# Rank and gather-index work of two batch groups due most of a batch sooner, order planned anew

## The chip, the cores and the metric

One core of one Trainium2 chip. The metric is device time in microseconds: the median of three runs of the kernel before was 818.91 us (818.41 to 819.88).

## The reference, cut to what matters

Sixteen batches `b` of 512 tokens with 512 features, and a context of 512 x 1024 for each batch.

```python
# x: (16, 512, 512), ctx: (16, 512, 1024), lens: (16, 512) int32
h     = rmsnorm(layernorm(x), g_res) @ W_in.T + b_in
u     = rmsnorm(ctx, g_init)[..., :512]            # scaled by constants
s     = scan over the tokens: s[t] = exp(-dt) * s[t-1] + u[t]
bidx  = cumsum(lens, axis=1) - 1                   # where a patch ends
mark  = zeros.at[bidx].set(1)
plug  = clip(cumsum(mark, axis=1) - 1, 0, 511)     # rank of each token's patch
x     = x + h + s[plug]                            # a gather by row
y     = layernorm(x);  yp = y shifted by one token
r     = sigmoid((mu_r*y + (1-mu_r)*yp) @ W_r.T)
k     = relu((mu_k*y + (1-mu_k)*yp) @ W_k.T) ** 2
out   = x + r * (k @ W_v.T)
```

The part that the change touches is `plug`: from the sorted end positions of a batch, the rank of every token, which is the row that the gather reads for it.

## The kernel before

**Tiles and stages.** A batch is four blocks `j` of 128 tokens, or four blocks `c` of 128 features. Each of the four products of a batch (`a` with W_in, `k`, `r`, `v`) is four groups of 12 matmuls of 128x128 by 128x512: float32 is split into a high and a low half, and a group sums high x high, high x low and low x high, four matmuls each. The names of the profile: `pa`, `pk`, `pr`, `pw` are the results of the four products in PSUM, `xh`, `m`, `ka` their operands in two halves, `cx` the context tiles that hold the scan, `pc` the carry between the blocks of the scan, `dr` the scan in DRAM, `x` the batch itself, `y` its second norm, `tr` that norm transposed, `pv` the mix with the token before, `sg` the sigmoid.

**Staging.** In period `i` the kernel computes `k`, `r` and `v` of batch `i`, the product `a` of batch `i+1`, and loads, squares and scans the context of batch `i+2`. For batch `b` the gather is four indirect transfers `x<-dr,plug` that GpSimd issues (`gather`, one for each `j`); they add rows of `dr` to `x[:, j]`. VectorE then adds `pa` (`a_end`), which also frees the PSUM bank of `pa`, and takes the second norm (`norm2`).

**Ranks.** `plugs(b0, n)` makes the index of `n` batches at once: the first batch alone, then batches 1 to 3, and 4 to 7, 8 to 11 and 12 to 15. For four batches it is: four one-hot comparisons `oh` on VectorE (128x512, each in a temporary tile of its own), 16 small matmuls that count (`cp<-ohj,oh`), four VectorE instructions that clip and sum (`bm`), one matmul with a triangle (`cp<-bm,small`), and three VectorE instructions that end in the integer index (`pf`, `pf`, `plug`). The groups of batches 8 and 12 are added to the program behind the store of batches 4 and 7.

**Order.** No instruction stands where the loops put it. `Plan` takes every piece with its engines, an estimated cost, what it reads and writes, and a due time `late`, which is worked back from its users and from the buffers. `SHIFT` adds a fixed number of microseconds to the due time of all pieces of a stage, named by kind and batch. `Plan.order` then runs a list schedule by these due times and its costs, and picks as it goes: which engine takes a piece that two engines can do (`LO`: the low half, a subtraction, on VectorE or on GpSimd), and which buffer a tile gets. There are 8 temporaries (`tmp`, 128x512), 16 operand tiles (`op`), 3 tiles for `x`, and PSUM is 4 banks for products (`ps`) and 4 for transposes (`tr`); the free buffer with the lowest number is taken. The order so found is then fixed on each engine:

```python
            if p.at is not None:
                p.late = p.at
            elif p.engines[0][0] == PE and p.due < INF:
                p.late = max(p.late, p.due - EASE)
            p.late += SHIFT.get(p.stage, 0.0)
```

Each engine works through its own queue in that order and waits at the head of it. Loads on SyncE carry one more wait, for a TensorE piece that stood some microseconds before them in the plan.

Of the kernel before, what the change touches and what calls it, by code (L numbers as in the profile page):

```python
# [289 lines left out]
class InOrder:  # L290
# [98 lines left out]
    ("sq", 4): 2.2,  # L389
    ("stat1", 4): 2.5,  # L390
    ("store", 4): -10.4,
}
ONLY = {
    ("rv", 0): 0,
# [939 lines left out]
```

## Time and profile before

| | |
|---|---|
| median of 3 runs | 818.91 us (818.41 to 819.88) |
| profiled execution, own time | 820.11 us |
| its span, first to last instruction | 818.3 us |
| granted TensorE clock, mean | 0.989 |
| TensorE matmul busy | 793.1 us (97%) |
| VectorE busy | 603.9 us (74%) |
| ScalarE busy | 485.1 us (59%) |
| GpSimd busy | 442.3 us (54%) |

In the profile PE is TensorE's matmuls and PEld its weight loads, DVE is VectorE, ACT ScalarE, POOL GpSimd, SP SyncE. Nearly all instructions have line 300, which is the helper that records them, so groups are told apart by the tiles that they write and read, with the numbers of batch and buffer left out. `x<-dr,plug` is the gather, `x<-bc` the transfer that adds the bias to `x`. The clock is given as a share of full speed. In the answers with a wait, the arrow names what ended it.

### The profile page before, as it was taken

The page shows a single profiled execution, that of the slowest core. Times are in us where ns is not written, and L with a number is a line of the kernel's source. Part 1 is how long each engine was busy: PE and PEld are TensorE (multiplying, and loading weights), DVE is VectorE, ACT ScalarE, POOL GpSimd, SP SyncE. Part 2 cuts the span into 40 slices and gives each one's busy share as a digit, 9 for nine tenths or more (in the row PEclk, how much of TensorE's full clock was granted, in tenths as well). Part 3 has the DMA queues.
Part 4 walks back from the last instruction along what each step waited for, and adds up shares of the span by engine and source line. Part 5 has one row for each costly group of instructions (what it writes and reads, how often), then busy time and mean ns, then how long its engine had stood idle before and what let it go on. Part 6 is the DMA issues. An engine that isn't in the chain of part 4 may idle for free.

```text
span 818.3 us, 11141 instructions
## 1 busy us (share of the span) xinstructions
PE 793.1 (97%) x3627; PEld 629.5 (77%) x3627; DVE 603.9 (74%) x1331; ACT 485.1 (59%) x950; POOL 442.3 (54%) x366
## 2 busy tenths in 40 slices
PE   7998998999999999999899999999989999999997
PEld 4776776877777888877678888887768888888885
DVE  6899798989789696777867678586966959564432
ACT  6937495555573757565476756647656565654550
POOL 2843675574767656552665566543566564561220
PEclk8999999999999999999999999999999999999999
DMA  9857485885685877673756866745577574430011
GB/s 322 269 91 260 101 236 144 283 224 155 142 241 155 175 200 194 168 217 111 208 126 171 224 155 208 153 168 146 150 216 170 199 139 170 91 80 16 2 52 51
DMA packets 52554, 134.69 MB, mean 165 GB/s; under 512 B 4752, under 2 KB 5264, under 8 KB 50576
## 3 DMA queue, kind: packets, MB, share of 16 engines
q1 hardware_dynamic: 35744, 102.39, 36.7%
q0 software_dynamic: 16608, 31.46, 23.8%
q8 instruction: 28, 0.46, 0.2%
q14 instruction: 30, 0.25, 0.1%
q10 hardware_dynamic: 144, 0.13, 0.0%
HBM read 85.73 MB, written 33.55 MB: 146 GB/s over the span
## 4 chain that ended last, share of the span: by engine, by line
PE 69%; DVE 13%; DMA 8%; issue 3%; POOL 3%; ACT 2%; SPq 0%; DVEq 0%; POOLq 0%; ACTq 0%
PE pk L300 18%; PE pr L300 17%; PE pw L300 17%; PE pa L300 14%; DMA x<-dr,plug 4%; DVE x L300 3%; PE tr L300 3%; DMA x<-x 3%; DVE cx L300 2%; DVE pv L300 2%; DVE sg L300 1%; PE pc L300 1%; DMA cx<-cx 1%; DMA out<-x 1%; POOL x L300 1%
## 5 line engine op out<-in xcount | busy, mean ns | idle before, releaser
L300 POOL TENSOR_TENSOR m<-pv,m 128x512 fp32r<-128x512 f32 x80 | 113.0, 1419 | 109.0 <-ACT m L300 50.4
L300 PE MATMUL pk<-m,whk 128*128 128x512 f32 x512 | 136.3, 401 | 6.8 <-DVE x L300 6.7
L300 PE MATMUL pa<-wha,xh 128*128 128x512 f32 x512 | 136.7, 404 | 4.9 <-DVE x L300 2.0
L300 PE MATMUL pw<-whv,ka 128*128 128x512 f32 x512 | 139.5, 399 | 0.4 <-ACT sg L300 0.4
L300 PE MATMUL pr<-whr,m 128*128 128x512 f32 x512 | 138.6, 397 | 0.0
L300 POOL DMA_INDIRECT x<-dr,plug x64 | 112.7, 1760 | 46.7 <-issue 15.7
L300 ACT ACTIVATE pv<-tr,om 128x384 f32<-128x384 f32 (+1 forms) x256 | 100.5, 487 | 41.6 <-PE tr L300 26.9
L300 DVE SCALAR_TENSOR_TENSOR pv<-tr,small,pv 128x511 f32<-128x511 f32 x128 | 95.0, 742 | 37.0 <-ACT pv L300 37.0
L300 PEld LDWEIGHTS pk<-m,whk 128*128 128x128 f32 x512 | 96.7, 191 | 33.0 <-DVE x L300 8.6
L300 PEld LDWEIGHTS pa<-wha,xh 128*128 128x128 f32 x512 | 96.8, 191 | 31.6 <-DVE x L300 3.2
L300 PEld LDWEIGHTS pr<-whr,m 128*128 128x128 f32 x512 | 95.2, 188 | 23.6 <-ACT kr L300 0.9
L300 PEld LDWEIGHTS pw<-whv,ka 128*128 128x128 f32 x512 | 94.6, 188 | 22.6 <-ACT sg L300 1.3
L300 ACT CAST m<-pv 128x512 fp32r<-128x512 f32 x128 | 76.3, 643 | 41.1 <-DVE pv L300 36.1
L300 ACT ACTIVATE sg<-pr 128x512 f32<-128x512 f32 x64 | 38.3, 600 | 96.4 <-PE pr L300 86.0
L300 DVE TENSOR_TENSOR ka<-kr,ka 128x512 fp32r<-128x512 f32 x52 | 39.8, 764 | 75.0 <-ACT ka L300 74.9
L300 ACT ACTIVATE y<-x,r 128x512 f32<-128x512 f32 x48 | 39.1, 815 | 73.0 <-DVE r L300 47.7
L300 DVE TENSOR_TENSOR sg<-pw,sg 128x512 f32<-128x512 f32 (+1 forms) x65 | 44.0, 678 | 41.6 <-PE pw L300 41.6
L300 ACT ACTIVATE junk<-cx 128x1024 bf16<-128x1024 f32 x64 | 67.5, 1055 | 7.4 <-DMA cx<-cx 7.1
L300 PE MATMUL pa<-wla,xh 128*128 128x512 f32 x256 | 71.1, 401 | 0.3 <-POOL wla L300 0.3
L300 PE MATMUL pk<-m,wlk 128*128 128x512 f32 x256 | 71.3, 403 | 0.0
L300 POOL TENSOR_TENSOR r<-r,mhalf 128x1 f32<-128x1 f32 x64 | 40.0, 627 | 57.2 <-DVE r L300 47.0
L300 PE MATMUL pw<-wlv,ka 128*128 128x512 f32 x256 | 70.5, 397 | 0.0
(116 smaller groups left out, 1276.8 us busy)
## 6 DMA issues: line engine op xcount, KB each, us to landing
cx<-cx SPq DMA_DIRECT2D x64, 512.0 KB, 6.0
dr<-cx SPq DMA_DIRECT2D x64, 256.0 KB, 4.4
out<-x SPq DMA_DIRECT2D x31, 512.0 KB, 2.7
x<-x SPq DMA_DIRECT2D x15, 1024.0 KB, 6.1
x<-bc POOLq DMA_DIRECT2D x14, 1024.0 KB, 8.1
raw<-xT SPq DMA_DIRECT2D x26, 512.0 KB, 6.1
wsa<-winT SPq DMA_DIRECT2D x2, 512.0 KB, 5.5
x<-x SPq DMA_DIRECT2D x4, 256.0 KB, 6.9
```

The source lines that it names most:

```text
L300: r = self._tc.keep_in_program_order(op(*args, **kwargs))
```

## The change

Two entries are added to `SHIFT`: all pieces of the rank and index work of batches 8 to 11 and of batches 12 to 15 get a due time 40 us sooner. No function changes, and no instruction is added or removed.

```diff
@@ SHIFT
     ("stat1", 4): 2.5,
     ("store", 4): -10.4,
+    ("plugs", 8): -40.0,
+    ("plugs", 12): -40.0,
 }
```

The plan is made anew with these due times, so other pieces change place too. As the two programs are built, TensorE's order is the same but for the 17 rank matmuls of each group. On VectorE, ScalarE, GpSimd and SyncE the order differs from period 5 to period 8 and again from period 9 to period 12, and is the same elsewhere. Ten subtractions move from VectorE to GpSimd (`m_1_3`, `ka_0` and `ka_1` of batches 6 and 10, `m_1_3` and `m_0_2` of batches 7 and 11; the first number is 1 for `k` and 0 for `r`, the last is `c`) and two from GpSimd to VectorE (`cl` of batches 8 and 12).

## The prediction

> **What bounds it now.** First the page: TensorE, and the chain is two thirds matmuls. A measurement of this kernel can tell about 0.2% (1.6 us) from no change.
>
> ```profile
> PE 793.1 (97%) x3627; PEld 629.5 (77%) x3627; DVE 603.9 (74%) x1331; ACT 485.1 (59%) x950; POOL 442.3 (54%) x366
> PE 69%; DVE 13%; DMA 8%; issue 3%; POOL 3%; ACT 2%; SPq 0%; DVEq 0%; POOLq 0%; ACTq 0%
> ```
>
> So only what stops TensorE counts. Stretches of 25 us show where that is, behind the first 275 us:
>
> ```profile
> core 0: us, PE busy (x) PEld busy (x) DVE busy (x) ACT busy (x) POOL busy (x), PEclk, DMA share, GB/s
> 375.00:400.00 25.00, 25.00 (x131) 20.14 (x130) 23.34 (x46) 13.37 (x29) 13.99 (x10) 1.00 0.50 133
> 400.00:425.00 25.00, 21.76 (x87) 17.11 (x86) 14.24 (x43) 15.81 (x27) 13.41 (x14) 0.93 0.76 204
> 425.00:450.00 25.00, 25.00 (x118) 20.44 (x117) 19.50 (x36) 13.80 (x29) 15.47 (x11) 1.00 0.60 152
> 600.00:625.00 25.00, 22.16 (x89) 17.43 (x88) 14.10 (x37) 15.88 (x28) 14.46 (x12) 0.93 0.63 158
> ```
>
> All other rows from 275 to 800 have 25.00 busy at clock 1.00. Both holes lie in the periods that prepare batches 8 and 12, whose ranks the change moves. Stretches of 2 us show the clock behind the first hole, then the timeline what leads to it:
>
> ```profile
> 410.00:412.00 2.00, 2.00 (x8) 1.56 (x8) 1.90 (x8) 2.00 (x4) 1.14 (x2) 0.73 0.85 289
> 412.00:414.00 2.00, 2.00 (x7) 1.51 (x6) 1.63 (x5) 1.94 (x4) 1.91 (x2) 0.50 0.31 119
> 414.00:416.00 2.00, 2.00 (x9) 1.63 (x8) 1.47 (x7) 1.97 (x5) 1.40 (x2) 0.91 0.00 0
> ```
>
> ```profile
> 388.08 1.21 DVE L300 CAST plug<-pf 128x16 int32<-128x16 f32 x1
> 389.58 1.70 POOL L300 DMA_INDIRECT x<-dr,plug  x1 [0.32 <-DVE plug L300]
> 399.34 1.55 POOL L300 DMA_INDIRECT x<-dr,plug  x1 [0.16 <-issue]
> 408.90 0.75 DVE L300 SCALAR_TENSOR_TENSOR x<-pa,rs,x 128x512 f32<-128x512 f32 x1 [3.70 <-DMA x<-dr,plug]
> 409.71 1.20 PE L300 MATMUL pk<-m,whk 128*128 128x512 f32 x4 [3.24 <-DVE x L300]
> ...
> 431.88 1.54 POOL L300 DMA_INDIRECT x<-dr,plug  x1 [0.17 <-issue]
> ```
>
> The index is ready at 389.3, the last gather goes out at 399.34 and lands 9.46 us later (the chain has that as one piece), VectorE adds `pa` only then, and TensorE waits for that PSUM bank. Batch 9, without rank work, has its four gathers out from 424.35 to 431.88, before its `pa` starts at 443.89. For batch 8, `pa` starts at 391.62: the first gather stands only 2.0 us before `pa`, not 19.5. The wait for the index itself is only 0.32 us; what costs is that the plan, expecting the index late, put the gathers behind subtractions on GpSimd.
>
> **Gain, step by step.** The period from one first `pr` matmul to the next is 47.21 us (419.75 to 466.96) and 47.22 in plain periods; 53.05 (366.70 to 419.75) and 52.95 (561.56 to 614.51) in the two with ranks. Excess: 5.84 + 5.74 = 11.58. Of it:
> - Idle: `pk` matmuls of 0.933 a four end at 406.30 and go on at 409.71, 3.41; at batch 12 601.47 to 604.47, 3.00.
> - Half clock behind it: nine fours take 10.04 where 9 x 0.933 = 8.39: 1.65 in each.
> - The rank matmuls, which stay: 382.60 to 386.95 holds four fours (3.73) in 4.35: 0.62 in each.
> - Rest: 0.16 and 0.47 (small waits for VectorE at `pa`).
>
> With the gathers out early, all but the 2 x 0.62 can go: 10.34. That they will be: in the order as built, all four stand directly behind the `sq` power of batch 9 (372.5 in this trace, some 2 us later by then), with one addition between, ahead of all `m` subtractions of batch 7. Batch 7's four with that addition took 9.3 us (322.89 to 332.2); so the fourth leaves at about 385 and, at the median 5.7 us, lands near 391, and its `pa` block ends at 403.5. The bias transfer before it (out at 362.39, 8.1 us) goes up to 3.2 us later, behind two `ka` subtractions; still 6 us clear.
>
> **What moves, and its cover.** The rank work now stands 38 us earlier.
> - Four one-hots, 0.69 each by the median (2.76): VectorE has a hole there, `4.01 <-ACT pv` before `pv` at 333.13. One has taken 1.78 against GpSimd; 3.85 still fits. Price 0; without the hole, 2.8 to 3.9 on VectorE.
> - Counting matmuls behind two fours of `pa`: bank free when VectorE has read `pw`, 344.46, against 345.44. Price 0, to 0.5.
> - `bm` 0.68 and `pf`, `plug` 0.50 unhindered (in this trace up to 1.64 and 1.94 while GpSimd ran): between `pa` additions. I follow VectorE with this trace's durations: `pa` of block 2 is added by 355.2 where TensorE needs the bank at 356.2, block 3 by 358.1 of 359.0. Price 0, to 1 each. The ScalarE reads of `pk` behind it end 0 to 0.9 before need; together I take 0.15 for each period.
> - Ten subtractions to GpSimd at 1.42 and two back: +11.4 in 94 us where it is half idle; `ka_0` and `ka_1` are done 8 us before `pw` reads them. Price 0. VectorE loses eight.
> - SyncE: the 1 MB load of `x` for batches 9 and 13 goes ahead of the four `dr` writes, not behind two; 3 us sooner. Price 0 (rival 1).
> - What is late next: `pc` now takes the bank of `pa` block 0, and has to wait for VectorE's addition. In batch 9 that ends at 447.73 where `pc` started at 447.62, so 0.2 each, bounds 0 and 0.5.
>
> Sum: 10.34 - 2 x 0.15 - 2 x 0.2 = 9.6. The profiled 820.11 becomes 810.5; the median, 1.2 lower, 818.91 - 9.6 = 809.3.
>
> **A rule beside the clock rows.** Idle stretches of 1.59 us (47.70) and 1.77 (132.64) are followed by full clock, those of 2.03 (66.08), 2.84 and 3.24 by half clock for some 3.4 us. So a hole of 2 us or more costs 1.65 more, a shorter one itself. [...]
>
> **Rivals.**
> 1. The load of `x` becomes the wait. VectorE now has two statistics of batch 9 (`st<-x`, 0.82 each) before its addition of `pa` block 3; before it was none, one in batch 9. By batch 9's times: `x` asked for at 448.33, landed 6.64 later (as at 349.92) at 455.0, two statistics and the 0.74 end at 457.4; the bank is needed at 458.57. At the 7.8 us of 385 to 410 it is level; at 10.1, the longest landing of anything into `x`, TensorE waits 2.3 + 1.65, twice: 7.9 back, 817.2. For it: at 356.59 VectorE did wait 0.78 for this load. Against: gathers and `dr` writes no longer share the queue then. At a wait of 1: 811.3.
> 2. The half clock is not the hole's doing but comes with these periods. The 2 x 1.65 then stays: 9.6 - 3.3 = 6.3, 812.6. Against: no period without a hole has it from 275 on.
> 3. The gathers wait for something else just as long (`dr`, the bias): 818.9. Against: `dr` was written by about 357 and GpSimd waited for the index alone.
> 4. Slower: the one-hots hold four of the eight temporaries from about 329 to 346. The mix of batch 6 then goes through two, one behind the other: `pv` 0.77, VectorE 0.79, cast 0.58, GpSimd 1.3 and hops, 4 us a trip, three trips from 332.3 in one buffer. VectorE's third `pv` stands before the `sg` product that frees the bank of `pa` block 0; by these trips that is done at 342.6, needed at 343.57. Beyond 1 us of lateness TensorE waits; the whole is slower once each wait is over 3.5 (with 1.65 of clock, twice, more than 10.3), so if trips take 5.5 instead of 4. At 6 us: 2 x 7.65 - 10.3 = 5, 823.9. Against: the longest subtraction of such a trip here adds 0.6.
>
> **How the numbers follow.** Forecast 78%; rival 1 10%, rival 2 4%, rival 3 3%, rival 4 5%. Faster by over 0.2%: 78 + 10 + 4 = 92%; the same 3%; slower 5%. Low end: all 10.34 and 0.8 of scatter (the runs before span 0.5 below to 1.0 above), 807.8. High end: rivals 1 at moderate waits and 2, and the prices at their upper bounds (2 x 2.2 more, 813.7), 814.0; about 15% stays outside.
>
> **What would show it.** Right: `pr` to `pr` about 48 in the two periods, no `pk` wait of 2 us or more, clock 1.00 in the rows of 400 and 600, the fourth gather out some 6 us before `pa`, the index some 38 us before its gather. Wrong: a TensorE wait behind `x<-x` (1), behind `sg` or `pv` near 344 or 534 (4), or a first gather that still waits (3).

## Result and profile after

The changed kernel takes 809.34 us (median of 4 runs, 808.58 to 810.34); the kernel before took 818.92 beside it (818.41 to 819.88). The ratio is 0.9879, with a 95% interval of 0.9864 to 0.9895: 9.6 us faster. The profiled execution is 808.87 us long, its span 807.1. First the page's row of busy times, then the answer for the stretches of 25 us (the columns as before), the rows that had the two holes and their neighbours:

```profile
PE 788.4 (98%) x3627; PEld 628.2 (78%) x3627; DVE 594.3 (74%) x1323; ACT 486.0 (60%) x950; POOL 453.1 (56%) x374
```

```profile
375.00:400.00 25.00, 24.34 (x113) 19.60 (x113) 20.96 (x43) 14.32 (x30) 18.55 (x14) 1.00 0.76 214
400.00:425.00 25.00, 25.00 (x113) 20.23 (x112) 14.46 (x38) 16.71 (x29) 17.31 (x14) 1.00 0.71 153
575.00:600.00 25.00, 24.46 (x105) 19.39 (x104) 19.37 (x50) 16.03 (x30) 18.31 (x17) 1.00 0.73 226
600.00:625.00 25.00, 25.00 (x117) 20.46 (x116) 14.75 (x28) 15.05 (x30) 14.41 (x10) 1.00 0.68 157
```

The rows at 400 and 600, which had 21.76 and 22.16 us of matmuls at clock 0.93, are full at 1.00. The rows at 375 and 575, which were full, now miss 0.66 and 0.54. The view of waits, asked for TensorE from 275 to 800, has one group left (total, times, longest), and the timeline shows its first instance and what stands before it:

```profile
PE pc L300 <- DVE x L300: 1.2, 2, 0.7
```

```profile
372.46 2.19 POOL L300 DMA_INDIRECT x<-dr,plug  x1 [0.18 <-issue]
...
380.74 1.55 POOL L300 DMA_INDIRECT x<-dr,plug  x1 [0.30 <-issue]
...
388.93 1.10 PE L300 MATMUL pa<-wha,xh 128*128 128x512 f32 x4
...
392.70 0.74 DVE L300 SCALAR_TENSOR_TENSOR x<-pa,rs,x 128x512 f32<-128x512 f32 x1
393.50 0.50 PE L300 MATMUL pc<-ch,scan_hi 128*128 128x512 f32 x1 [0.66 <-DVE x L300]
```

The four gathers of batch 8 now go out from 372.46 to 380.74, so the last starts 8.2 us before `pa`; before, it started 7.7 us behind it. Behind 275 us no matmul waits for a gather's landing any more. What is late next is `pc`, which has the bank of `pa` block 0 and waits until VectorE has read it.

The timeline also shows the rank work in its new place, a batch earlier:

```profile
328.09 2.61 DVE L300 TENSOR_TENSOR oh<-hj,small 128x512 f16<-128x512 f32 x4 [1.45 <-POOL x L300]
...
339.23 0.68 DVE L300 TENSOR_TENSOR sg<-pw,sg 128x512 f32<-128x512 f32 x1
...
342.97 0.55 PE L300 MATMUL cp<-ohj,oh 128*128 128x4 f16 x16
...
346.12 0.17 DVE L300 CAST plug<-pf 128x16 int32<-128x16 f32 x1
```

The table gives the periods from one first `pr` matmul to the next; a plain one is 47.22. It has four of the seven periods from the one that starts at 319.44 before and at 316.97 after. The seven sum to 342.29 before and 333.52 after, 8.77 less:

| period | before | after | what is left over 47.22 |
|---|---|---|---|
| ranks now stand here (first group) | 47.26 | 47.83 | 0.61, the rank matmuls |
| prepares batch 8 | 53.05 | 48.14 | 0.92, the wait of `pc` (0.66 shown as idle) |
| ranks now stand here (second group) | 47.38 | 47.87 | 0.65 |
| prepares batch 12 | 52.95 | 48.02 | 0.80, the wait of `pc` (0.54 shown as idle) |

The wait of `pc` takes more than the idle time in the brackets: the first `pc` starts 0.83 us behind the pace of the matmuls ahead of it (390.80 + 8 x 0.233 = 392.67, against 393.50), and the second follows it by 0.33, where 0.23 is usual.

### The profile page after: what moved, and what is told of

Its sections match the earlier page's. It is cut to its first block, busy times and chain, and to the rows that moved or that the text cites. A ratio compares the mean times of both kernels' runs of the same rounds, so it can differ in the third digit from the quotient of the medians.

```text
span 807.1 us, 11158 instructions
## 1 busy us (share of the span) xinstructions
PE 788.4 (98%) x3627; PEld 628.2 (78%) x3627; DVE 594.3 (74%) x1323; ACT 486.0 (60%) x950; POOL 453.1 (56%) x374
## 5 line engine op out<-in xcount | busy, mean ns | idle before, releaser
L300 POOL TENSOR_TENSOR m<-pv,m 128x512 fp32r<-128x512 f32 x86 | 120.9, 1414 | 121.3 <-ACT m L300 59.7
L300 PE MATMUL pk<-m,whk 128*128 128x512 f32 x512 | 133.8, 396 | 0.6 <-DVE x L300 0.6
L300 DVE TENSOR_TENSOR ka<-kr,ka 128x512 fp32r<-128x512 f32 x48 | 35.9, 749 | 76.3 <-ACT ka L300 76.2
L300 PE MATMUL pr<-wlr,m 128*128 128x512 f32 x256 | 70.3, 396 | 0.0
```

Source lines behind the costliest of these rows:

```text
L300: r = self._tc.keep_in_program_order(op(*args, **kwargs))
```

## Experiments

The theory under test, P: the gathers stood too late in GpSimd's queue, and the two holes and the half clock behind them followed from that. Against it stand R, that it is the place of the rank work which counts; rival 2, that the half clock belongs to these periods and not to the hole; and S, that the two groups act only together. The edits are shown against the change, except where the kernel before is named.

### Ranks in their old period, gathers early

```diff
-    ("plugs", 8): -40.0,
-    ("plugs", 12): -40.0,
+    ("plugs", 8): -10.0,
+    ("plugs", 12): -10.0,
```

> Due times 10 us sooner instead of 40. As built, the ranks of batch 8 stay in the same period (counted behind the third product group of r, not one period ahead), so VectorE's crowded stretch before pa keeps them; but the four gathers stand ahead of three of the four m subtractions that were before them. Theory P (the hole comes from the gathers' place on GpSimd): no pk wait of 2 us, some 8.5 to 10 us faster than before, 809 to 810.5. Rival R (the gain comes from taking the rank work out of that stretch of VectorE and TensorE): at most 2 us faster, 817 or more.

Measured: 809.96 us, ratio 0.9885 (0.9867 to 0.9903); the kernel before took 819.45 beside this and the next two. The rank matmuls stay in the old period, as the timeline shows, yet the last gather is out before `pa`, and no wait of 2 us is left:

```profile
374.07 0.44 PE L300 MATMUL cp<-ohj,oh 128*128 128x4 f16 x12 [0.62 <-DVE sg L300]
...
379.31 1.70 POOL L300 DMA_INDIRECT x<-dr,plug  x1 [2.95 <-DVE plug L300]
...
388.18 1.82 POOL L300 DMA_INDIRECT x<-dr,plug  x1 [0.16 <-issue]
...
388.59 1.10 PE L300 MATMUL pa<-wha,xh 128*128 128x512 f32 x4
```

Here GpSimd even waits 2.95 us for the index, and TensorE does not feel it. VectorE has two subtractions more than in the kernel before, so the ten that the change takes from it are not what closes the holes. What this variant loses against the change (335.46 us in the seven periods, 1.94 more) shows as waits of the counting matmuls for `sg`, 1.4 us in two, and for `kr`, 0.5 twice. R falls: the rank work still stands in the period that prepares batch 8, and 6.83 of the 8.77 us are there.

The run does not show that the index may come as late as before. It is ready 16.0 us behind the first `pr` of its period here (379.02), where it was 22.6 (389.29 in the kernel before), and the first gather leaves as soon as it is there. In the kernel before the first gather could have left at most 0.32 us sooner, wherever it stood in the queue. Only the gaps between the gathers could have closed: from first to fourth 9.76 us, against 7.53 for batch 9. That was not tried.

### Ranks early, GpSimd's old order

The change, but GpSimd is held to the order of the kernel before. That puts the ten subtractions back on VectorE, and the other engines are planned anew around it.

```diff
-ORDER = {}
+ORDER = {"gpsimd": (18, 20, 109, 75, 77, 43, 79, 81, 44,
...
```

> The change's due times, with GpSimd held to the order it had before: the index is ready a period sooner, the gathers leave where they did. Theory P: both holes stay, with pk waits near 3 us and the half clock behind them; only the 0.3 us wait for the index goes, so 818 to 819. Rival R (the rank work itself was in the way): half of the gain or more, 814 or less. Rival I (the wait for the index was the cause): all of the gain, 809 to 810.

Measured: 817.25 us, ratio 0.9972 (0.9959 to 0.9984). The index is ready long before, and the gathers (timeline) start with 0.18 and 0.17 us of `issue` ahead of them, no wait for the index; still they are out late, and the holes are there:

```profile
396.10 1.55 POOL L300 DMA_INDIRECT x<-dr,plug  x1 [0.16 <-issue]
...
406.60 0.75 DVE L300 SCALAR_TENSOR_TENSOR x<-pa,rs,x 128x512 f32<-128x512 f32 x1 [3.72 <-DMA x<-dr,plug]
407.40 2.08 PE L300 MATMUL pk<-m,whk 128*128 128x512 f32 x4 [2.90 <-DVE x L300]
...
602.45 1.20 PE L300 MATMUL pk<-m,whk 128*128 128x512 f32 x4 [2.22 <-DVE x L300]
```

So three quarters of the gain go if GpSimd's order is put back (2.2 us of 9.6 are left by the medians; by the seven periods, 341.19 us, 1.1 of 8.8). An early index is not enough: the gathers' place in GpSimd's queue makes the holes by itself. With the run before, this shows P for the gathers: early, they give the gain even with the ranks in the old period; late, they take it away even with the index ready. Whether early places alone would do, with the index as late as it was, is not shown. A surprise stands beside it: the hole of 2.22 us was followed by full clock (row of 600 to 625 at 1.00), so that period took 50.42 us, where the first took 53.42. The holes were also shorter (2.90 and 2.22, against 3.24 and 2.84 in the same view of the kernel before). P had expected neither.

### The hole filled with matmuls

The kernel before, with 48 matmuls of 128x128 into an unused bank behind the first `k` product of batches 7 and 11. Their result is not read; they keep TensorE busy where it had been idle.

```diff
+NFILL = 48
...
+            for _ in range(NFILL):
+                e.matmul(S[n][:, :P], ones, ones, start=True, stop=True)
...
+        if d == 1 and b in (7, 11):
+            fill(b, due - 0.5)
```

> The kernel before, with 48 extra matmuls of 128x128 (about 3.1 us) into a free transpose bank behind the first k product of batches 7 and 11, where TensorE otherwise stands idle; all other orders as before. Theory P with the clock row (the idle stretch brings the half clock): the bank is waited for as long, but the clock stays at 1.00, 2 x 1.65 = 3.3 us faster, 815.6. Rival 2 (the half clock belongs to these periods whatever TensorE does): 818.9, clock rows of 0.93 as before.

Measured: 818.17 us, ratio 0.9986 (0.9974 to 0.9998). The answer for stretches of 25 us has clock 1.00 at both places, so rival 2 falls: take most of the idleness away and the half clock is gone.

```profile
400.00:425.00 25.00, 23.00 (x134) 18.13 (x133) 13.75 (x42) 15.82 (x27) 13.13 (x14) 1.00 0.76 201
600.00:625.00 25.00, 23.47 (x135) 18.53 (x134) 14.23 (x38) 16.02 (x28) 14.20 (x12) 1.00 0.62 156
```

But the 3.3 us that P had expected did not come. By the medians it was 1.3, and in the trace, which is of one of the two slowest of its 12 runs, nothing: the seven periods take 342.88 us, against 342.29. Where the 1.3 comes from is not known. The timeline shows what took the gain:

```profile
406.12 2.85 PE L300 MATMUL fill<-ones 128*128 128x128 f16 x48
410.05 1.20 PE L300 MATMUL pk<-m,whk 128*128 128x512 f32 x4 [1.07 <-DVE x L300]
416.16 1.20 PE L300 MATMUL pk<-m,whk 128*128 128x512 f32 x4 [0.24 <-ACT kr L300]
422.07 0.58 ACT L300 ACTIVATE kr<-pk 128x512 f32<-128x512 f32 x1
422.70 1.20 PE L300 MATMUL pr<-whr,m 128*128 128x512 f32 x4 [0.68 <-ACT kr L300]
```

The late addition makes ScalarE late too. In both traces ScalarE starts its read of the last `pk` bank (`kr`) 12.83 us behind the start of VectorE's addition (408.90 to 421.73 before, 409.24 to 422.07 here). At half clock TensorE had been slow enough for these reads to keep up. At full clock it reaches the banks early and waits 0.24 and 0.68, and the period behind takes 48.16 instead of 47.21. From the addition to the end of that period it is 58.06 us before and 57.98 here. So in these traces the half clock cost nothing beside ScalarE's lateness, which the hole had brought as well.

### Each group alone

```diff
     ("plugs", 8): -40.0,
-    ("plugs", 12): -40.0,
```

> Only the ranks of batches 8 to 11 are due 40 us sooner; those of batches 12 to 15 keep their place. Theory P (the late gathers make a hole, in each of the two periods by itself): the first hole goes and the second stays, with its half clock. By the change's own trace the first period falls from 53.05 to 48.14 us and the one before it rises from 47.26 to 47.83, so 4.3 us of gain, 814.3 to 815.0. Rival S (the two moves help each other, through buffers that carry over from batch 8 to batch 12): under 3 us of gain, over 815.9, or the second period changes although its order does not.

Measured: 814.70 us, ratio 0.9942 (0.9922 to 0.9962), the kernel before at 819.58 beside it: 4.9 us. The first hole is gone (48.15), the second stands with 3.21 us of idle time (52.90).

```diff
-    ("plugs", 8): -40.0,
     ("plugs", 12): -40.0,
```

> Only the ranks of batches 12 to 15 are due 40 us sooner. Theory P: the second hole alone goes: that period from 52.95 to 48.02 us, the one before it from 47.38 to 47.87, 4.4 us of gain, 814.2 to 815.0, and the first period stays at about 53.0 with its hole of some 3.4 us and clock 0.93 in its row. Rival S: under 3 us, over 815.9. The gains of the two halves add up to the whole by P (9.6 by the medians), within 1 us.

Measured: 813.97 us, ratio 0.9940 (0.9916 to 0.9964): 5.6 us. The other way round: 54.59 and 48.03. The two sum to 10.5; the change itself, beside them, gave 10.2:

> The change itself, beside its halves and the variant with the bank on the same chip: 809.3, half of the gain from each of the two groups. TensorE waits 0.5 to 0.7 us for the bank of pc in the periods of batches 9 and 13 and nowhere else behind 275 us.

Measured: 809.34 us (808.53 to 810.23), ratio 0.9879 (0.9854 to 0.9903). The halves add up and neither needs the other; S falls. The periods repeat (47.84, 48.13, 47.87, 48.00), and so does the wait of `pc`: 1.2 in two.

In the profiled execution of the variant with the second group alone the remaining hole was dearer than before: 54.59 against 53.05. Stretches of 2 us show why:

```profile
406.00:408.00 2.00, 0.00 (x0) 0.00 (x0) 0.34 (x1) 0.00 (x0) 0.00 (x0) 0.97 1.07 387
408.00:410.00 2.00, 1.53 (x4) 1.24 (x5) 1.93 (x7) 1.37 (x3) 0.37 (x1) 0.50 0.91 352
410.00:412.00 2.00, 2.00 (x6) 1.57 (x5) 1.91 (x6) 1.94 (x4) 2.00 (x3) 0.50 0.58 221
412.00:414.00 2.00, 2.00 (x6) 1.56 (x5) 1.66 (x6) 2.00 (x5) 1.31 (x2) 0.50 0.00 0
414.00:416.00 2.00, 2.00 (x8) 1.58 (x8) 0.31 (x6) 1.94 (x5) 1.94 (x2) 0.82 0.03 8
```

A row of 2 us at mean clock c, taken as a mix of 1.00 and 0.50, holds 4(1-c) us of half clock: 0.12, three times 2.00, and 0.72, together 6.84. In the kernel before the rows 0.73, 0.50 and 0.91 give 1.08, 2.00 and 0.36: 3.44. The same hole (3.59 us of idle time here, 3.24 there) brought 6.84 us of half clock in one execution and 3.44 in the other, and the period with the 6.84 was 1.5 us longer; 0.6 us of the 6.84 lay within the hole itself.

### The wait of `pc`

At 44 us instead of 40 the plan gives `pc` of batches 9 and 13 a free bank.

```diff
-    ("plugs", 8): -40.0,
-    ("plugs", 12): -40.0,
+    ("plugs", 8): -44.0,
+    ("plugs", 12): -44.0,
```

> Due times 44 us sooner instead of 40. The gathers come out as early, and as built the carry pc of batches 9 and 13 gets another bank than pa block 0 of batches 8 and 12. Theory P: the pc waits of 0.66 and 0.54 go, and nothing else comes: 1.2 to 1.5 us below the change, 807.9. Rival (the plan trades one small wait for another): 809.3 with other waits of the same sum.

Measured: 808.74 us (808.14 to 809.69), ratio 0.9866 (0.9845 to 0.9887). The view of waits has no wait of TensorE from 275 to 800; the two periods take 47.22, and the seven 331.78, which is 1.74 less than the change. It was run once more beside the change:

> 44 us sooner instead of 40, in which plan pc of batches 9 and 13 takes a bank that is free, not that of pa block 0. If the wait for that bank costs what it shows (periods of 48.14 and 48.02 against 47.22, together 1.7 us by the traces), this runs 1.7 us under the change beside it, 807.6. If that wait only stands in for another one behind it (as the half clock did when the hole was filled), the two are within 0.6 us.

Measured: 808.81 us (807.14 to 810.77) against 809.34 (808.53 to 810.23); the seven periods take 331.79 against 333.50. So behind 317 us the wait of `pc` is worth 1.7 us, the whole of the 0.92 and 0.80 in the table, in two traces each. In the medians only 0.5 to 0.6 of it was seen, and the ranges overlap; whether this variant is faster than the change as a whole is not settled. Its two profiled executions lost more ahead of 317 us, where nothing was moved: `tr` waited 2.06 and 2.61 us for `y` near 130, against 0.4 and 1.1 in those of the change. Whether that is chance was not settled either.

## Why the prediction was right, step by step

- **The cause.** Right that the gathers' late issue made the holes, and that an index in time alone would not close them. Too narrow where the wait of 0.32 us is read as all that the index cost: GpSimd's other work ended at 389.26 and the index came at 389.29, so both held the first gather back, and the change moved both. No run has early places with the index as late as it was.
- **Idle time and half clock, 3.41 + 3.00 + 2 x 1.65.** Gone, as forecast. The step behind it, that a hole of 2 us or more costs 1.65, was wrong as a rule: 2.22 us brought no half clock, 2.90 and 3.59 brought 6.84 us of it (last section). In the kernel before the two holes had brought 3.44 each. Nor are the 2 x 1.65 a price of their own: with the holes filled and the clock full, the seven periods were no shorter.
- **Rank matmuls, 2 x 0.62, which stay.** 0.61 and 0.65.
- **Cover of the rank work, priced at nothing.** Held. The one-hots stood in VectorE's hole, behind 1.45 us of waiting for GpSimd; the second `sg` product was done at 339.91, 1.2 before the `pa` that needs its bank (341.10), where the forecast had 1.0 in rival 4. The later `pa` additions ended 1.0 and 1.4 before need. `pf` and `plug` took 0.16 to 0.17 each; the cast had taken 1.21 in its old place.
- **Lateness of ScalarE and VectorE, 2 x 0.15.** No wait of that kind shows, and with the wait of `pc` gone (44 us) the two periods are plain, 47.22. Nothing of it came.
- **`pc` waits for a bank, 2 x 0.2.** The term that was mis-sized: 0.92 and 0.80 in the periods (0.66 and 0.54 as idle time), above the upper bound of 0.5. The forecast took VectorE's place from batch 9, where the addition ended 0.11 behind the need; here VectorE ran a `pv` mix until 392.66 and could begin the addition only at 392.70.
- **The sum.** By the traces 8.77 in the seven periods, against 9.6: `pc` took 1.3 more than forecast, and the 0.3 for ScalarE and VectorE was not spent. That the medians show 9.6 all the same is not explained by the mechanism. Two things vary from execution to execution: the first `pr` of the table starts anywhere from 315.80 to 320.57 in the ten traces, though no order changes ahead of it, and a hole like the old ones brings 3.4 us of half clock or 6.8. The runs do not part them. So the exact hit is partly luck; the mechanism's own worth in the traces is about 8.8.
- **The places named.** The fourth gather was out 8.2 us before `pa` (forecast 6), the index 26 us before its gather (forecast 38, which left out that the gathers move forward too; they did by 17). The bias transfer was to land 6 us clear of them; by the forecast's own figures it was 2 (362.39 + 8.1 + 3.2 = 373.7, with the first gather behind the `sq` power that ends near 375.6). No gather of batch 8 waited for it.
- **Rivals.** 1: the statistics behind the load of `x` ran unwaited at 400.97, and the last `pa` addition ended at 403.30, 1.25 before need. One reason given against it was not one: the profile has the gathers on GpSimd's queue (`POOLq`) and the load of `x` on SyncE's (`SPq`), so they share none. 2 fell by the filled hole. 3 by the trace. 4 did not show, and its example leaves out its own 1 us of slack: trips of 6 us make a wait of 5, so 2 x 6.65 - 10.3 = 3.0 and 821.9, not 823.9. A variant with fewer free temporaries was not tried, so only the trace speaks against it.

## What to carry to other kernels

When an engine with a queue in order issues the transfers, ask at which place in the queue they stand, and not only when their input is ready: here a wait for the index of 0.32 us stood in front of a loss of 5 us in each period, since a plan that expected the index late had put other work first. A short wait at the head of a queue does not say that the producer is in time; it says that two things came at once. Moving the producer paid only because the plan then moved the issue too; 10 us of lead did nearly as much as 40. And before an idle stretch is closed in part, look at what it covers: with the clock back but the gathers still late, all of the expected gain went, by the traces, to the next engine's lateness.

## What the runs showed of the hardware

The half clock behind a hole depends on more than its length. A hole near 66 us is the same in all ten traces (`pa` waits 2.01 to 2.03 us for `x`, in a part of the program that no variant changes). In six of them the row of 50 to 75 has clock 0.93, in four 1.00. Here is the change itself, the wait in the timeline and the row for the stretch of 25 us, in its first trace

```profile
65.82 1.72 PE L300 MATMUL pa<-wha,xh 128*128 128x512 f32 x4 [2.01 <-DVE x L300]
```

```profile
50.00:75.00 25.00, 22.38 (x107) 16.96 (x106) 23.82 (x47) 15.43 (x34) 7.06 (x7) 0.93 0.78 213
```

and in its second:

```profile
66.04 1.20 PE L300 MATMUL pa<-wha,xh 128*128 128x512 f32 x4 [2.02 <-DVE x L300]
```

```profile
50.00:75.00 25.00, 22.15 (x115) 16.49 (x114) 24.83 (x48) 15.42 (x34) 7.29 (x8) 1.00 0.77 210
```

Holes of 2.06 and 2.22 us went without half clock; 2.61, 2.84, 3.21 and 3.24 brought 3.40 to 3.44 us of it, 2.90 and 3.59 brought 6.84 each. It set in 2.0 to 4.5 us behind the start of the hole; in the kernel before at 66.18, 410.93 and 605.49, with holes that ended at 66.08, 409.71 and 604.47.

What decides whether a hole is followed by half clock, and for how long, the runs do not show: the ends of matmuls are modelled in the profile, which gives the lengths of the holes, and no run set the length or the start of a hole on purpose. So a hole of 2 to 4 us brought no half clock, some 3.4 us or some 6.8 us of it. The 3.4 us cost TensorE 1.65 us in the kernel before (nine fours in 10.04, where 8.39 is usual); the 6.84 at the hole of 3.59, of which 0.6 lay within the hole, cost about 3 by an estimate, half of the other 6.24. What the kernel feels of that can be less, as the filled holes show.
